# Two graph networks on one core: the order of every engine's work is written out by hand

## The chip, the cores and the metric

The kernel runs on one core of a Trainium2 chip. The metric is the device time of one execution in microseconds (us). A core has five engines with a queue each: PE (matmul), DVE (vector), ACT (scalar), POOL (gathers and scatters by index) and SP (plain DMA issues; ACT issues some too). Each works through its own queue; semaphores tie them together.

## The reference, cut to what matters

There are 6250 nodes with 64 features and 200000 edges sorted by target. First a one-layer graph network updates the nodes, then an edge MLP and three attention layers follow.

```python
# first network, per target node over its edges
e      = leaky_relu(cat([pre_w * z[src], z[dst]]) @ att_w)       # z = x @ Wa
alpha  = softmax of e over the edges of a node
h      = sum(alpha * z[src]);  max_feat = max(pre_w * x[src] @ Wg);  mean_feat = mean(pre_w * x[src])
x      = layernorm(x + sigmoid(cat([x, max_feat, mean_feat]) @ gate_w) * h)
# second network
edge_attr = relu(ln(edge_embed) @ eW1 + eb1) @ eW2 + eb2          # 64 -> 256 -> 64 for every edge
for l in range(3):
    hh    = ln(x)
    alpha = softmax over the edges of (q(hh[dst]) * (kn(hh[src]) + ke(edge_attr)))    # 8 heads of 8
    agg   = sum(alpha * (vn(hh[src]) + ve(edge_attr)))
    gate  = sigmoid(agg @ Wih + hh @ Whh)
    x     = x + (agg + gate * (hh @ Wself - agg)) @ Wout
    x     = x + relu(ln(x) @ mW1) @ mW2
x = layernorm(x + ln(x_second))
```

## The kernel before

The nodes are sorted by degree and cut into 49 blocks (NB) of 128, one node a partition. Block b has CAPS[b] edge slots a node (50 down to 21). There are two stages.

**Stage 1** does the first network and the edge MLP, block by block. `meet` fetches a block's index data (me), own rows (ow) and edge features (xe) by indirect DMA and builds masks. `fetch` gathers one source row a slot (L662, tile g, four buffers). `absorb` is the first network: the products and reductions of the gathered rows on DVE (a_part, L841 and L856), the exponential on ACT (L850), the node update and layernorm, then `prepare`, which normalizes the new rows for layer 0 and makes the key and value rows (p_kv, L561 to L565). `place_rows` writes those rows to the table `tab` by indirect DMA (L537). `even` layernorms the edge features on DVE (f_sm L672, f_sq L678) and stores them. `select` finds, for each node, one edge in each of 16 "windows" of the source numbers (NW = 16), and lists the other edges (LCAPS[b], 40 down to 14). Window edges are later read by one-hot matmuls. It builds the one-hots in four sets: a matmul broadcasts (L743), ACT copies (s_bc, L746), DVE compares three times (s_oh, L749), and SP stores (oh_d, L750). `order` puts a block's edges into the new order on PE: SP loads the stored features (f_xs, L763), DVE makes a selection matrix (f_mv, L775), PE multiplies (f_tr, L781), ACT copies (f_xt, L784). `features` is the edge MLP: f_ph (L818) on PE, f_hid (L821) on ACT, f_pe (L800) on PE, ea (L804) on ACT, stored to ea_d (L805).

**Stage 2** runs the three layers over the blocks in the order ORDER. A layer first loads the whole table's bf16 parts for the window matmuls (ftb, seven DMAs on ACT's queue, L958). `fetch1` loads a block's one-hots (ohl), edge terms (eal), transposed node rows (hv), and node rows (b_x), and gathers the rows of the non-window edges (L986). `attend` takes the edge terms (L1008), the gathered rows through an identity matmul (L1013), or the window rows through one-hots (L1022), into b_pk in PSUM, eight edges a time. ACT copies them out (b_k L1026, b_v L1029), and DVE makes scores (L1031, L1032), softmax and the weighted sum (L1033 to L1043). Then the chain of the node update follows: flip, gate (L1068 to L1075), output projection, layernorm (b_h), flip (p_pm L523), MLP (L1088 to L1094), the new row b_x (L1095), and `prepare` for the next layer. Layer 2 writes the output instead (L1107). The next layer's gathers read a table whose rows must all be written.

Both stages sit in a context `schedule_with_timeline_sim=True`: a scheduler decides, from modelled times, in which order each engine gets its instructions; the program text fixes only what depends on what. The buffer pools decide what may be in flight. In PSUM of stage 1 there are two banks each for f_tr and p_pm, a two-bank f_ph tile, and one bank for f_pe.

Of the kernel before, what the change touches and what calls it, by code (L numbers as in the profile page):

```python
# [9 lines left out]
F32 = mybir.dt.float32  # L10
# [8 lines left out]
H = 8  # L19
# [402 lines left out]
def passes(ctx, tc, ins, out, meta_d, t0_d, own_d, ident, row_f, ones, norm_c, st_i, id_i, off, end, has, hash_, rdeg,  # L422
# [118 lines left out]
    def prepare(wk, mps, w, b, xb, i):  # L541
# [3 lines left out]
        norm(wk, hn, xb)  # L545
        pt = mps.tile([D, P], F32, name="p_pm")
# [7 lines left out]
        if b == 0:  # L554
            nc.sync.dma_start(hd[LB][:, LN:P], ht[:, :SPARE])
        pm = mps.tile([P, W1], F32, name="p_pm")
        nc.tensor.matmul(pm, ht, w["wc"][:, D : 3 * D], start=True, stop=True)
        kv = wk.tile([P, WT], F32, name="p_kv", bufs=3)
        part = kv[:, W1:].bitcast(BF).rearrange("p (k d) -> p k d", k=3)
        rest = wk.tile([P, W1], F32, name="p_rest")  # L560
        nc.scalar.copy(kv[:, :W1], pm)  # L561
        nc.scalar.copy(part[:, 0], pm)
        nc.vector.tensor_tensor(rest, pm, part[:, 0], ALU.subtract)
        nc.scalar.copy(part[:, 1], rest)
        nc.vector.tensor_tensor(part[:, 2], rest, part[:, 1], ALU.subtract)  # L565
# [4 lines left out]
    with tc.tile_pool(name="e1", bufs=1) as wp, tc.tile_pool(name="e_g", bufs=4) as gp, \  # L570
# [3 lines left out]
            tc.tile_pool(name="e_tr", bufs=2, space=PSUM) as tps, \  # L574
            tc.tile_pool(name="e_h", bufs=1, space=PSUM) as hps, tc.tile_pool(name="e_e", bufs=1, space=PSUM) as eps2, \
            tc.tile_pool(name="e_p", bufs=2, space=PSUM) as mps, tc.tile_pool(name="e_f", bufs=1, space=PSUM) as fps:
# [25 lines left out]
        xss = [wp.tile([P, D // 4, D], F32, name=f"f_xs{i}") for i in range(6)]  # L602
# [18 lines left out]
        def meet(b):  # L621

            c, ce = CAPS[b], CAPE[b]
# [6 lines left out]
            xe = xp.tile([P, c, D], F32, name="xe")  # L630
            nc.gpsimd.indirect_dma_start(out=xe.rearrange("p c d -> p (c d)"), out_offset=None, in_=ins["edge_attr_64"][:],
                                         in_offset=bass.IndirectOffsetOnAxis(ap=st_i[:, b : b + 1], axis=0))
            kk, wt = row_f[:, :c], me.bitcast(F32)[:, :, 1]
# [20 lines left out]
            got[b] = dict(me=me, ow=ow, xe=xe, vm=vm, ivm=ivm, am=am1, wg=wg, si=si)  # L654

        def fetch(b):
            m = got[b]
            m["g"] = []
            for k0, k1 in cuts(CAPS[b], b == ORDER[-1]):
                g = gp.tile([P, CH, F0], F32, name="g0")  # L660
                for k in range(k0, k1):
                    nc.gpsimd.indirect_dma_start(  # L662
                        out=g[:, k - k0, :], out_offset=None, in_=t0_d[:],
                        in_offset=bass.IndirectOffsetOnAxis(ap=m["si"][:, k : k + 1], axis=0))
                m["g"].append((k0, k1, g))

        def even(b):
# [5 lines left out]
            nc.vector.tensor_scalar(mr, sm[:, 0], 1.0 / D, None, ALU.mult)  # L673
            nc.vector.tensor_tensor(xe, xe, mr.unsqueeze(2).to_broadcast([P, c, D]), ALU.subtract)
            for k0 in range(0, c, 12):
                k1 = min(k0 + 12, c)
                sq = wk.tile([P, 12, D], F32, name="f_sq")
                nc.scalar.activation(sq[:, : k1 - k0], xe[:, k0:k1], AF.Square)  # L678
                nc.vector.tensor_reduce(sm[:, 1, k0:k1], sq[:, : k1 - k0], AX.X, ALU.add)
# [4 lines left out]
            nc.sync.dma_start(xd_d[b][:], xe)  # L684

        def select(b):
# [12 lines left out]
            nc.vector.tensor_tensor(v, t[:, 0], vm, ALU.mult)  # L699
            me = w1p.tile([P, NW, c], F32, name="s_m")  # L700
# [4 lines left out]
            nc.vector.tensor_reduce(sel, me, AX.X, ALU.max)  # L705
            nc.vector.tensor_scalar(f_sm, sel, 1.0, None, ALU.max)
            nc.vector.tensor_tensor(me, me, f_sm.unsqueeze(2).to_broadcast([P, NW, c]), ALU.is_equal)
            ch, lv, pos = t[:, 1], t[:, 2], t[:, 3]
            nc.vector.tensor_reduce(ch, me.rearrange("p w k -> p k w"), AX.X, ALU.max)
            nc.vector.tensor_sub(lv, vm, ch)  # L710
# [9 lines left out]
            m["tg"] = tg  # L720

            lf = wk.tile([P, lc], F32, name="s_lf")
            for l0 in range(0, lc, 12):
# [5 lines left out]
                nc.vector.tensor_reduce(lf[:, l0 : l0 + n], li, AX.X, ALU.add)  # L729
# [166 lines left out]
        for i in range(NB + 3):  # L896
            if i < NB:
                meet(ORDER[i])
# [911 lines left out]
```

## Time and profile before

| | |
|---|---|
| time, median of 3 runs | 8684.05 us (8675.6 to 8702.06) |
| time of the profiled execution | 8682.54 us |
| its span | 8680.7 us, so 1.84 us lie around it |
| granted PE clock, mean | 0.798 |
| PE busy | 6156.6 us (71%) |
| DVE busy | 5618.3 us (65%) |
| POOL busy | 5163.6 us (59%) |
| ACT busy | 2467.9 us (28%) |
| first gather of layer 0, 1, 2 | 3660, 5410, 7111 us |

The shares are averages over stages that work differently. A table by stage and the waits of that stage say more than the totals. In a line of waits, the engine and line that stood still come first, then what ended the wait, its total in us, the number of times, and the longest. A wait of an engine that isn't the bottleneck costs nothing by itself.

### The profile page before, as it was taken

The page shows a single profiled execution, that of the slowest core. Times are in us where ns is not written, and L with a number is a line of the kernel's source. Part 1 is how long each engine was busy: PE and PEld are TensorE (multiplying, and loading weights), DVE is VectorE, ACT ScalarE, POOL GpSimd, SP SyncE. Part 2 cuts the span into 40 slices and gives each one's busy share as a digit, 9 for nine tenths or more (in the row PEclk, how much of TensorE's full clock was granted, in tenths as well). Part 3 has the DMA queues.
Part 4 walks back from the last instruction along what each step waited for, and adds up shares of the span by engine and source line. Part 5 has one row for each costly group of instructions (what it writes and reads, how often), then busy time and mean ns, then how long its engine had stood idle before and what let it go on. Part 6 is the DMA issues. An engine that isn't in the chain of part 4 may idle for free.

```text
span 8680.7 us, 151284 instructions
## 1 busy us (share of the span) xinstructions
PE 6156.6 (71%) x58020; PEld 4136.1 (48%) x58020; DVE 5618.3 (65%) x13393; ACT 2467.9 (28%) x5210; POOL 5163.6 (59%) x5441
## 2 busy tenths in 40 slices
PE   2455556566565566678778886889888868888897
PEld 1222223233232233355656664566666646666676
DVE  6677667777566576555655665566656646677777
ACT  1233334334333343422222221222222212222222
POOL 4555445555444444377776671777777627777775
PEclk6677777777676677788888887888888868888998
DMA  5444344454343344365555663556666635556664
GB/s 120 121 113 132 109 121 134 124 141 123 110 116 109 108 123 120 105 182 142 146 139 137 150 146 89 142 146 149 152 147 154 143 96 140 139 146 149 152 163 107
DMA packets 965727, 1146.71 MB, mean 132 GB/s; under 512 B 665160, under 2 KB 713109, under 8 KB 957961
## 3 DMA queue, kind: packets, MB, share of 16 engines
q1 hardware_dynamic: 504569, 642.88, 23.9%
q0 software_dynamic: 180144, 412.30, 23.6%
q10 hardware_dynamic: 280288, 81.76, 3.9%
q8 instruction: 466, 7.63, 0.4%
q14 instruction: 260, 2.13, 0.1%
HBM read 899.50 MB, written 236.89 MB: 131 GB/s over the span
## 4 chain that ended last, share of the span: by engine, by line
PE 22%; POOL 14%; DVE 9%; issue 7%; DMA 5%; ACT 1%; ACTq 0%; SPq 0%; POOLq 0%; DVEq 0%
POOL g L986 13%; PE b_pk L1022 7%; PE b_pk L1013 5%; PE b_pk L1008 5%; DMA g<-tab,fidx 3%; DVE b_ag L1043 2%; DVE b_k L1031 2%; DVE b_al L1032 1%; DMA hv<-ht_d 1%; DVE b_v L1042 1%; PE p_pm L1088 1%; PE p_pm L1094 1%; PE p_pm L1092 0%; PE b_qe L997 0%; DVE n_t L501 0%
## 5 line engine op out<-in xcount | busy, mean ns | idle before, releaser
L986 POOL DMA_INDIRECT g<-tab,fidx x3426 | 3273.1, 955 | 1154.5 <-issue 991.7
L662 POOL DMA_INDIRECT g<-ft_d,si x1596 | 1530.0, 959 | 1652.6 <-DVE a_part L856 1152.7
L1022 PE MATMUL b_pk<-ftb,ohl 128*128 128x128 bf16 x21609 | 1409.5, 225 | 63.1 <-DMA ftb<-tab 49.8
L1022 PEld LDWEIGHTS <-ohl 128*128 128x128 bf16 x21609 | 1299.4, 101 | 142.4 <-issue 81.3
L1013 PE MATMUL b_pk<-g,fident 128*128 128x512 f32 (+3 forms) x2148 | 1091.8, 629 | 253.1 <-DMA g<-tab,fidx 227.2
L1008 PE MATMUL b_pk<-fwkv,eal 64*128 64x128 f32 x11556 | 1047.2, 313 | 224.8 <-ACT b_v L1026 223.4
L781 PE MATMUL f_tr<-f_mv,f_xs 128*64 128x40 f32 (+11 forms) x12544 | 576.3, 261 | 817.2 <-DVE f_mv L775 575.8
L1008 PEld LDWEIGHTS b_pk<-fwkv,eal 64*128 64x128 f32 x11556 | 856.6, 210 | 531.8 <-ACT b_v L1026 262.2
L818 PE MATMUL f_ph<-f_xt,fw 64*128 64x448 f32 (+3 forms) x2320 | 736.6, 718 | 471.5 <-ACT f_hid L821 467.5
L781 PEld LDWEIGHTS f_tr<-f_mv,f_xs 128*64 128x64 f32 x12544 | 564.5, 177 | 1024.1 <-DVE f_mv L775 583.0
L1026 ACT COPY b_k<-b_pk 128x512 f32<-128x512 f32 (+3 forms) x753 | 412.1, 547 | 1994.5 <-PE b_pk L1013 1067.5
L1043 DVE TENSOR_REDUCE b_ag<-b_v 128x64 f32<-128x2624 f32 (+18 forms) x147 | 654.6, 4453 | 265.4 <-PE p_pm L523 262.6
L1031 DVE TENSOR_TENSOR b_k<-b_k,b_qe 128x1024 f32<-128x1024 f32 (+11 forms) x402 | 436.4, 1105 | 528.8 <-ACT b_k L1029 233.7
L800 PE MATMUL f_pe<-f_hid,fw 128*64 128x448 f32 (+3 forms) x2320 | 677.7, 666 | 49.6 <-ACT ea L804 25.8
L821 ACT ACTIVATE f_hid<-f_ph,fb 128x896 f32<-128x896 f32 (+3 forms) x580 | 566.6, 977 | 467.6 <-PE f_ph L818 416.0
L1013 PEld LDWEIGHTS b_pk<-g,fident 128*128 128x128 f32 x2148 | 412.3, 221 | 545.2 <-issue 376.8
L818 PEld LDWEIGHTS f_ph<-f_xt,fw 64*128 64x128 f32 x2320 | 217.6, 229 | 702.1 <-ACT f_hid L821 632.6
L749 DVE TENSOR_SCALAR s_oh<-s_bc,f_parts 128x512 bf16<-128x512 f16 x588 | 185.0, 367 | 508.0 <-DMA oh_d<-s_oh 484.2
L784 ACT ACTIVATE f_xt<-f_tr,feg 128x304 f32<-128x304 f32 (+11 forms) x392 | 240.6, 615 | 936.4 <-PE f_tr L781 916.5
L775 DVE TENSOR_TENSOR f_mv<-s_tt,e_fac 128x608 f32<-128x608 f32 (+11 forms) x392 | 311.5, 810 | 217.3 <-PE f_tr L781 202.0
L1032 DVE TENSOR_REDUCE b_al<-b_k 128x128 f32<-128x1024 f32 (+11 forms) x402 | 435.0, 1102 | 3.4
L537 POOL DMA_INDIRECT tab<-p_kv,id_i x147 | 147.4, 1002 | 482.8 <-DVE p_kv L565 356.6
(359 smaller groups left out, 7947.0 us busy)
## 6 DMA issues: line engine op xcount, KB each, us to landing
ohl<-oh_d SPq DMA_DIRECT2D x588, 384.0 KB
eal<-ea_d SPq DMA_DIRECT2D x174, 512.0 KB
oh_d<-s_oh SPq DMA_DIRECT2D x196, 384.0 KB
g<-tab,fidx POOLq DMA_INDIRECT x3426
eal<-ea_d SPq DMA_DIRECT2D x93, 384.0 KB
eal<-ea_d SPq DMA_DIRECT2D x66, 448.0 KB
ea_d<-ea ACTq DMA_DIRECT2D x130, 224.0 KB
g<-ft_d,si POOLq DMA_INDIRECT x1596
```

The costliest lines, as they stand in the source:

```text
L662: nc.gpsimd.indirect_dma_start(out=g[:, k - k0, :], out_offset=None, in_=t0_d[:], in_offset=bass.IndirectOffsetOnAxis(ap=m["si"][:, k : k ...
L781: nc.tensor.matmul(pv[r * D : (r + 1) * D, j], xs[4 * j0 // D][:, (j0 + j) % (D // 4), :], mv[:, j, :, r::2], start=True, stop=True)
L800: nc.tensor.matmul(pe[h * D : (h + 1) * D, :w], w2[:, s, :], hid[s][:, h, :w], start=(s == 0), stop=(s == 1))
L818: nc.tensor.matmul(ph[:, h, :w], w1[r, s * P : (s + 1) * P], xf[r, e0 * D : e1 * D], start=True, stop=True)
L821: nc.scalar.activation(hid[s][:, :, :w], ph[:, :, :w], AF.Relu, bias=b1[:, s : s + 1])
L986: nc.gpsimd.indirect_dma_start(out=g[:, k - k0, :], out_offset=None, in_=tab.rearrange("n (k d) -> (n k) d", d=D), in_offset=bass.Indirect ...
L1008: nc.tensor.matmul(pk[:, j % 2, j // 2, :], ea[r, e, :], w["wkv"][r], start=(j < 2), stop=False)
L1013: nc.tensor.matmul(pk[:, h, :m, :], ident, g[:, u0 - k0 + h : u0 - k0 + n : 2, :], start=False, stop=True)
L1022: nc.tensor.matmul(pk[:, h, j, :], o, tbh[:, cl + NW * u, i, :], start=False, stop=(j == m - 1 and u == us[-1] and i == 2))
L1031: nc.vector.tensor_tensor(k, k, q.unsqueeze(1).to_broadcast([P, k1 - k0, D]), ALU.mult)
L1032: nc.vector.tensor_reduce(al[:, k0:k1], k.rearrange("p k (h d) -> p k h d", h=H), AX.X, ALU.add)
L1043: nc.vector.tensor_reduce(a, vv.rearrange("p k d -> p d k"), AX.X, ALU.add)
```

## The change

Both stages are now inside `tc.manual_schedule()`: every engine gets its instructions in the order of the program text. The text is rewritten so that this order is meant. In stage 1, `absorb`, `even`, `masks` (split off from `meet`) and `select` become generators that yield after a piece, with a weight in us. An iteration has eight steps (STEPS), and each lays down an eighth of the weight, drawn from two jobs (the absorb of block i-2; the even, masks and select of blocks i-1 and i), one `order` step, and two steps of the edge MLP.

```diff
-            tc.tile_pool(name="e_tr", bufs=2, space=PSUM) as tps, \
-            tc.tile_pool(name="e_h", bufs=1, space=PSUM) as hps, tc.tile_pool(name="e_e", bufs=1, space=PSUM) as eps2, \
-            tc.tile_pool(name="e_p", bufs=2, space=PSUM) as mps, tc.tile_pool(name="e_f", bufs=1, space=PSUM) as fps:
+            tc.tile_pool(name="e_tr", bufs=1, space=PSUM) as tps, \
+            tc.tile_pool(name="e_h", bufs=2, space=PSUM) as hps, tc.tile_pool(name="e_e", bufs=1, space=PSUM) as eps2, \
+            tc.tile_pool(name="e_p", bufs=1, space=PSUM) as mps, tc.tile_pool(name="e_f", bufs=1, space=PSUM) as fps, \
+            tc.manual_schedule():
...
-        xss = [wp.tile([P, D // 4, D], F32, name=f"f_xs{i}") for i in range(6)]
+        xss = [wp.tile([P, D // 4, D], F32, name=f"f_xs{i}") for i in range(4)]
...
+        STEPS = D // JB
+        meet(ORDER[0])
+        for i in range(NB + 3):
+            bs = [ORDER[i - k] if 0 <= i - k < NB else None for k in range(4)]
+            if i < NB:
+                meet_features(bs[0])
+            if i + 1 < NB:
+                meet(ORDER[i + 1])
+            jobs = []
+            if bs[2] is not None:
+                jobs.append([absorb(bs[2]), 0.0, 25.0])
+            second = ([even(bs[1])] if bs[1] is not None else []) + ([masks(bs[0])] if bs[0] is not None else []) \
+                + ([select(bs[1])] if bs[1] is not None else [])
+            if second:
+                jobs.append([chain(*second), 0.0, 26.0])
+            total, done = sum(j[2] for j in jobs), 0.0
+            mlp = [features(bs[3], 1) if bs[3] is not None else iter(()), features(bs[2], 0) if bs[2] is not None else iter(())]
+            for s in range(STEPS):
+                b = bs[2]
+                if b is not None:
+                    mv = got[b]["mv"]
+                    if s < STEPS - 1:
+                        aim(b, (s + 1) * JB)
+                half = s * 2 // STEPS
...
+                next(mlp[half], None)
+                while jobs and (done < total * (s + 1) / STEPS or s == STEPS - 1):
...
+                if b is not None:
+                    order(b, s * JB, mv)
+                next(mlp[half], None)
...
+                if s % 2:
+                    n = 4 * (i - 2) + s // 2 + 2
+                    if 0 <= n < 4 * NB:
+                        bring(n)
+            fetch()
+            if bs[1] is not None:
+                aim(bs[1], 0)
+            place_rows(1)
+        place_rows()
```

`bring` holds the f_xs loads, `aim` the f_mv, `order` the f_tr matmuls and the f_xt copy. `fetch` lists the gathers of a block's parts in order and issues as many as tiles are free: a tile counts as free behind the second reduction in `absorb` that reads it, and `fetch` is called there and at the end of an iteration. `place_rows(1)` keeps the last block's rows for the next iteration. The end of `select` reads:

```diff
+                bc = wk.tile([P, 4, P], F16, name="s_bc")
+                nc.scalar.copy(bc, pb)
+                yield 0.2
+                oh = wk.tile([P, 4, 3, P], BF, name="s_oh")
+                for u in range(3):
+                    nc.vector.tensor_scalar(oh[:, :, u, :], bc, parts[:, u : u + 1], None, ALU.is_equal)
+                nc.sync.dma_start(oh_d[b][:, w0 * 3 * P : (w0 + 4) * 3 * P], oh.rearrange("p w u n -> p (w u n)"))
```

In stage 2, `attend` is cut into functions: `sums` (b_pk and its copies, one group), `scores`, `soft`, `values`, `turned`, `gate`, `update`, `updated`, `turned2`, `hidden`, `close`, `more` (the pieces of `prepare`). An iteration takes the sums of block b, the softmax and gate of the block before (b1), the update of b2 and the rest of `prepare` of b3.

```diff
+            for _ in range(3):
+                load()
+            for _ in range(4):
+                load_oh(), gather()
+            for b in ORDER[:2]:
+                ms[b] = begin(b)
+            for i in range(NB + 4):
+                b, b1, b2, b3 = [ORDER[i - k] if 0 <= i - k < NB else None for k in range(4)]
...
+                do(b1, soft)
+                do(b2, updated)
+                if i + 2 < NB:
+                    ms[ORDER[i + 2]] = begin(ORDER[i + 2])
...
+                steps = [lambda: (do(b3, more), do(b1, values)), lambda: (do(b3, more), do(b2, turned2)),
+                         lambda: (do(b3, more), do(b2, hidden)), lambda: (do(b3, more), do(b2, close), do(b1, turned)),
+                         lambda: do(b1, gate), lambda: (do(b2, more), do(b1, update))]
+                done = 0
+                for j, (k0, k1, u0, u1) in enumerate(groups):
+                    if u0 == k0:
+                        m["k"] = wk.tile([P, CL, D], F32, name="b_k", bufs=3)
+                    sums(b, m, k0, k1, u0, u1)
+                    if u1 == k1:
+                        scores(m, k0, k1)
+                        load()
+                        if k0:
+                            gather()
...
+                    while done < len(steps) * (j + 1) // len(groups):
+                        steps[done]()
+                        done += 1
+                for f in steps[done:]:
+                    f()
+                place_rows()
+                put()
```

Smaller edits: the two small copies of p_kv read the SBUF tile instead of PSUM; the MLP's two p_pm tiles become one; groups of sums are balanced in size (a part of 10 edges is two groups of 6 and 4, not 8 and 2); hv has four buffers instead of three, b_x and xv five instead of three; the transposes of `order`'s target list move into `select`.

## The prediction, made before the change was run

> **What bounds the kernel now.** I first read the top of the page: no engine is busy throughout, so the bound differs by stage.
>
> ```profile
> span 8680.7 us, 151284 instructions
> ## 1 busy us (share of the span) xinstructions
> PE 6156.6 (71%) x58020; PEld 4136.1 (48%) x58020; DVE 5618.3 (65%) x13393; ACT 2467.9 (28%) x5210; POOL 5163.6 (59%) x5441
> ...
> PEclk6677777777676677788888887888888868888998
> ```
>
> The timeline of gathers gives the borders. The first network (stage 1) runs from about 240 to 3660 us, where the first row gather of layer 0 starts; the layers follow to 5407, 7108 and 8668. The table by stage, with two stretches of stage 1 and then the three layers, reads (window, then length, PE, PEld, DVE, ACT, POOL busy, granted clock, DMA share, GB/s):
>
> ```profile
> 1736.00:2170.00 434.00, 274.35 (x2582) 140.71 (x2582) 327.31 (x849) 174.18 (x280) 225.27 (x237) 0.76 0.48 132
> 2604.00:3038.00 434.00, 231.07 (x2184) 119.89 (x2180) 260.31 (x752) 140.99 (x241) 185.90 (x194) 0.69 0.39 108
> 3660.00:5407.00 1747.00, 1392.98 (x13464) 1044.75 (x13461) 1002.30 (x2077) 429.24 (x1117) 1137.98 (x1190) 0.85 0.56 139
> 5410.00:7108.00 1698.00, 1400.65 (x13192) 1057.28 (x13192) 1013.20 (x2041) 415.38 (x1097) 1140.83 (x1191) 0.84 0.58 141
> 7111.00:8668.00 1557.00, 1331.65 (x13009) 1010.55 (x13008) 1097.20 (x2580) 363.09 (x901) 1140.84 (x1191) 0.88 0.60 145
> ```
>
> In stage 1 DVE is busiest, at 75% in a good stretch and 60% in a bad one. What it and POOL wait for there (total, times, longest, 220 to 3600 us):
>
> ```profile
> POOL g L662 <- DVE a_part L856: 1152.7, 43, 47.1
> PE f_tr L781 <- DVE f_mv L775: 566.5, 64, 41.7
> DVE s_oh L749 <- DMA oh_d<-s_oh: 473.0, 51, 43.4
> DVE f_sm L672 <- DMA xe<-in_edge_attr_dram,st_i: 292.1, 31, 12.9
> ```
>
> A ring shows: gathers wait for DVE to free a gather tile, DVE stands up to 43 us at a one-hot build for a store queued on SP behind others, and SP's next f_xs load waits its turn. The start of each block's gathers gives the period: 356.46 to 3523.21 us over 44 blocks, 72.0 each, in good stretches 65.1 (1773.5 to 1968.7 is three blocks), in bad ones up to 108.
>
> In the layers POOL issues 1142 row gathers, 0.955 us each and 0.3 behind it, so 1.257 x 1142 = 1435 us, and 49 table writes at about 1.3 (64): a floor of 1500. It stands still beyond that for some 250, 200 and 60 us in layers 0, 1, 2, most at the end of a layer (6860 to 7120 us):
>
> ```profile
> POOL tab L537 <- DVE p_kv L565: 126.5, 8, 27.7
> POOL tab L537 <- DVE b_gt L1075: 44.1, 2, 23.2
> ```
>
> The last sums of layer 1 end at 7023.6, its last table row is written at 7107.8: 84 us of update chains, one after another, about 15.6 us apart, before the next layer's gathers may read.
>
> [...] the 43 us stall at L749 held all later DVE work. So a hand order is a real change, and an instruction that waits blocks those below it. [...]
>
> **Stage 1, part by part.** Removed nothing large: the same 588 one-hot builds, 12544 f_tr and 2320 f_ph matmuls, 1596 gathers. Moved:
>
> (a) Gathers go behind masks and each second a_part reduction, a full iteration ahead. POOL's work is 33.6 x 1.257 + about 4 = 46 us of a block, beside DVE. The 1152.7 us wait mostly had cover on DVE, so I give it no price of its own.
>
> (b) f_xs loads, two issues of about 3.4 us a quarter-block on SP, are brought two steps ahead, past the one-hot stores; two tiles fewer (six to four) are the price. SP's sum is some 38 us a block (eight such issues, four stores of 2.1, small ones), hidden behind DVE if no store waits at its head.
>
> (c) xe is asked for an iteration earlier: 292.1 us of DVE wait, 6 a block, go; POOL's gathers stand ahead of it by 41 us at most, less than an iteration.
>
> (d) DVE in program order. Its busy time in a block is 327.31 / 434 x 65.1 = 49. There were 849 / 434 x 65.1 = 127 operations; in the trace an independent follower starts 82 ns before its predecessor ends, a dependent one 34 ns after it (medians), a difference of 0.116. A hand order puts dependent ones together: at most 127 x 0.116 = 15, at least 0. I take 6: 55.
>
> (e) New stall: the last step of a block holds all four one-hot sets, 12 builds at 0.367. s_oh has two buffers and is freed by its oh_d store, 2.1 us of issue and about 3 of landing on SP, and each set waits for a PE broadcast and ACT copy on the single p_pm bank. Queued behind it: the next f_mv on DVE, so f_tr on PE. Two of four sets wait about 3.3 each: 6.5 (0 to 15).
>
> (f) Other in-order waits (softmax's exp between two DVE operations, f_mv for f_tr): 4 (0 to 12).
>
> So 55 + 6.5 + 4 = 65 us a block, DVE-bound and regular. Beside it, from the same stretch scaled to a block: PE 274.35 / 434 x 65.1 = 41, ACT 26, POOL 46 from (a). 49 x 65 = 3185, with about 90 for the three thinner iterations of start and drain 3275, against 3420: **145 gained** (-150 to +490).
>
> **The layers, part by part.** The update of a block (norm, flips, gate, MLP, close, table row) is cut into six pieces laid between the next blocks' groups of 8 sums; loads and gathers run four tiles ahead. PE per block: 147 window matmuls at 58 ns are 8.5, L1008 1.16 per eight edges, L1013 1.98, updates 6.7: 24 to 27. POOL: 52 us for a block of 40 edges, 29 for 22, 19 for 14. So POOL sets the pace for the first 29 blocks (764 gathers and 29 writes: 999 us); the middle dozen take 324 at about 27, the last eight 25.5 each by PE: 204. Sum 1527; start and drain I put at 80: the first gather-to-sum latency and a drain of three chained update stages, about 45 instead of 84. So **1610 a layer**. Layer 0: 1747 to 1610, +137; layer 1: 1698 to 1610, +88; layer 2: 1557 to about 1587, -30, since it has neither tail and already runs within 4% of POOL's floor. **195 gained** (0 to 330). The low end is a PE-paced 29 us in the small blocks, which adds 45 a layer, and a tail as long as now. p_kv's copies from SBUF, the merged p_pm tile and the balanced groups are single instructions beside POOL: zero, and if PE is the pace less than 0.5 us a block (25 a layer).
>
> **Sum.** 8682.54 (profiled run: span 8680.7 and 1.84 around it; 1.5 under the median 8684.05) - 145 - 195 = 8342, so **8340**. A measurement of this kernel can tell 0.3%, 26 us, from no change.
>
> **The rivals.**
> 1. *Stage 1 reaches DVE's floor.* No set stalls, more overlap: 58 a block, so 49 x 58 + 90 = 2932, 488 gained, beside the same 195. For it: the good stretch above runs at 65 with waits in it. Against: single banks, and four sets in a row. 8682 - 683 = 8000.
> 2. *Slower: the one-hot step blocks DVE.* In a strict order a store landing late on SP, behind f_xs loads of 3.4 us each, holds s_oh, then f_mv, then f_tr, then the single f_tr bank. The break-even is 340 / 49 = 7 us a block above mine, 72. With 75 a block stage 1 takes 3675 + 90, 345 more than now; less 195 it ends at 8830. For it: 43 us stalls of just this wait now. Against: f_xs is asked for earlier and in an order that never waits on a later store.
> 3. *The layers gain nothing:* PE in order waits on ACT's b_k and b_v copies (254 and 223 us in total now), what the tails give is spent there, and stage 1 comes out at 71. About 8680.
>
> **How the numbers follow.** My forecast 0.55 (8340, its own range 8150 to 8560), rival 1 0.29, rival 2 0.12, rival 3 0.04. Faster 0.84, same 0.04, slower 0.12. The range 7930 to 8670 takes in rival 1 and leaves out rival 2.
>
> **What would show it.** Right: the wait of L662's gathers for a_part falls from 1152.7 to under 300 in total, xe's to near nothing; block starts come every 63 to 67 us, evenly; s_oh still waits on its store, 200 to 400 in total, in runs of less than 10; the first layer's gather starts near 3515; from the last sums to the last table row takes about 45. Wrong: a period over 72 with s_oh or f_mv ahead of the idle; layers longer than 1650 with PE's waits on ACT ahead of POOL.

## The result, and the profile after

The changed kernel takes 8546.1 us (median of 4 runs, 8539.47 to 8553.86) where the kernel before took 8683.98 in the same runs: a ratio of 0.9839, with a 95% interval of 0.9821 to 0.9857. It is 138 us faster; 340 were forecast. The profiled execution took 8539.47 us around a span of 8537.4.

The top of the page after:

```profile
span 8537.4 us, 150270 instructions
## 1 busy us (share of the span) xinstructions
PE 6224.1 (73%) x58044; PEld 4258.2 (50%) x58044; DVE 6013.9 (70%) x13393; ACT 2476.6 (29%) x5234; POOL 5161.1 (60%) x5439
```

PE, ACT and POOL are busy about as long as before. DVE's busy time rose by 396 us (5618.3 before), though it has as many instructions. In stage 1 the order does this, not the new text: a later run (e6) gives that text back to the scheduler, and DVE is busy 2297 us in the stage, where the same text by hand (e1) has 2563. In program order dependent operations stand next to each other and overlap less. From 240 us to the first gather of layer 0 the durations of DVE's operations add up to 2749 us before and 2781 after, and overlap took 412 us off that before, 222 after. Of the neighbours on DVE that are under 0.3 us apart (220 to 3600 us), 3247 now read the tile that the one ahead has just written, where it was 910; these start 35 ns after its end (34 before), and those that read and write other tiles 82 ns before it (medians, 82 before).

The table by stage of the changed kernel (window, length, busy time of PE, PEld, DVE, ACT, POOL, granted clock, DMA share, GB/s). The windows run from one first gather to the next, so they are stage 1 and the three layers:

```profile
240.00:3626.00 3386.00, 2073.09 (x17987) 1031.63 (x17987) 2558.97 (x6279) 1246.06 (x2018) 1634.07 (x1705) 0.71 0.46 120
3626.00:5260.00 1634.00, 1354.24 (x13222) 1052.40 (x13218) 1061.44 (x2073) 415.90 (x1109) 1140.45 (x1191) 0.86 0.58 147
5260.00:6899.00 1639.00, 1362.17 (x13200) 1061.67 (x13200) 1060.10 (x2045) 412.15 (x1105) 1140.96 (x1191) 0.85 0.59 148
6899.00:8537.00 1638.00, 1349.34 (x13053) 1060.62 (x13053) 1171.34 (x2580) 359.16 (x909) 1140.73 (x1191) 0.83 0.57 139
```

| gained, us | forecast | measured |
|---|---|---|
| stage 1 (first gather of layer 0 at 3660.2, now 3625.6) | 145 | 34.6 |
| layer 0 (1750.2, now 1635.1) | 137 | 115.1 |
| layer 1 (1700.6, now 1638.8) | 88 | 61.9 |
| layer 2 to the end of the span (1569.6, now 1637.9) | -30 | -68.3 |

So 110 us are missing in stage 1, and 86 in the layers. The waits of stage 1 after (engine and line, releaser, total, times, longest; 220 to 3600 us):

```profile
POOL g L679 <- DVE wx L663: 1026.5, 41, 42.8
...
DVE p_kv L569 <- ACT p_kv L567: 190.3, 42, 8.2
...
DVE s_oh L791 <- DMA oh_d<-s_oh: 167.1, 79, 13.4
...
PE f_tr L825 <- DMA f_xs<-xd_d: 123.2, 17, 15.1
...
DVE p_rest L566 <- ACT p_kv L563: 107.8, 40, 3.5
```

DVE's wait for xe is gone (292.1 before), and that for the one-hot stores fell from 473.0 to 167.1. In their place two other waits have grown: DVE now stands 298 us for ACT's copies p_kv, in the making of the table rows. Of these the kernel before has only one worth a line, and a small one (220 to 3600 us):

```profile
DVE p_rest L563 <- ACT p_kv L562: 7.3, 4, 4.1
```

What the totals hide shows in the start of each block's node update, a_gm, once a block. Over the whole stage the blocks come every 71.6 us before and every 70.1 after. By the block's width (CAPS, slots a node) the mean distance to the block before is:

| width | 43 | 41 | 38 | 37 | 35 | 34 | 33 | 32 | 31 | 30 | 29 | 28 |
|---|---|---|---|---|---|---|---|---|---|---|---|---|
| before, us | 105 | 110 | 79 | 94 | 67 | 72 | 65 | 63 | 86 | 62 | 80 | 63 |
| after, us | 89 | 109 | 75 | 87 | 70 | 69 | 68 | 67 | 75 | 65 | 72 | 63 |

The blocks with a prime width (43, 41, 37, 31, 29) are slow in both kernels. At most other widths from 35 down the changed kernel is the slower one. SP's timeline of the changed kernel, first in blocks of width 31, then of width 33 (start, duration, line, what is issued, how many in a row):

```profile
2332.77 0.34 SPq L792 DMA_DIRECT2D oh_d<-s_oh  x1
2333.21 1.91 SPq L796 DMA_DIRECT2D oh_d<-s_o  x1
2335.21 5.04 SPq L792 DMA_DIRECT2D oh_d<-s_oh  x3
2340.35 22.57 SPq L805 DMA_DIRECT2D f_xs<-xd_d  x4
2363.03 8.13 SPq L712 DMA_DIRECT2D xd_d<-xe  x1
2371.25 11.18 SPq L805 DMA_DIRECT2D f_xs<-xd_d  x2
2382.95 7.59 SPq L944 DMA_DIRECT2D x_d<-a_x  x1
```

```profile
1918.13 4.36 SPq L792 DMA_DIRECT2D oh_d<-s_oh  x3
1922.58 3.65 SPq L805 DMA_DIRECT2D f_xs<-xd_d  x4
1943.56 0.34 SPq L712 DMA_DIRECT2D xd_d<-xe  x1
1943.99 1.21 SPq L805 DMA_DIRECT2D f_xs<-xd_d  x2
```

Four f_xs loads keep SP for 22.57 us at width 31 and for 3.65 at width 33. In the first the queue is busy without a break, and even the store of one small tile (x_d, 0.3 us elsewhere) is held for 7.6. The mean of one f_xs issue by width, over the whole stage: 43: 8.2, 41: 9.1, 37: 6.5, 31: 5.4, 29: 5.0, 23: 4.4; 38: 3.8, 34: 3.6; all others 0.5 to 1.7. The slow ones are the prime widths, and 34 and 38 somewhat. A load of width 31 has 31 x 16 rows of 256 bytes, 127 KB, and where four loads come in a row the later issues stand 6.9 to 7.8 us each, which is 16 to 18 GB/s; at 34 slots the mean is 3.6. The single packets of SP's queue in the trace agree. During four loads in a row at widths 29, 31, 37 and 43, at most 71 packets of 256 bytes pass in a us (18 GB/s) and never more than two are under way at once; at 34 and 38 it is 142 in a us and four at once; at 33 it is 392 to 540 in the densest us, with 12 to 16 under way. Why the width does this the trace does not show.

### The profile page after: what moved, and what is told of

The parts are those of the page before. It is cut to its first block, busy times and chain, and to the rows that moved or that the text cites. A ratio compares the mean times of both kernels' runs of the same rounds, so it can differ in the third digit from the quotient of the medians.

```text
span 8537.4 us, 150270 instructions
## 1 busy us (share of the span) xinstructions
PE 6224.1 (73%) x58044; PEld 4258.2 (50%) x58044; DVE 6013.9 (70%) x13393; ACT 2476.6 (29%) x5234; POOL 5161.1 (60%) x5439
## 5 line engine op out<-in xcount | busy, mean ns | idle before, releaser
L679 POOL DMA_INDIRECT g<-ft_d,si x1596 | 1527.7, 957 | 1625.1 <-DVE wx L663 1026.5
L1101 PE MATMUL b_pk<-ftb,ohl 128*128 128x128 bf16 x21609 | 1375.8, 229 | 19.4 <-DMA ftb<-tab 19.4
L1101 PEld LDWEIGHTS <-ohl 128*128 128x128 bf16 x21609 | 1325.0, 104 | 65.5 <-issue 41.4
L1093 PE MATMUL b_pk<-g,fident 128*128 128x384 f32 (+3 forms) x2172 | 1028.8, 601 | 219.9 <-DMA g<-tab,fidx 180.5
L844 PE MATMUL f_pe<-f_hid,fw 128*64 128x448 f32 (+3 forms) x2320 | 710.7, 700 | 595.1 <-ACT ea L848 594.9
L1105 ACT COPY b_k<-b_pk 128x512 f32<-128x512 f32 (+2 forms) x753 | 404.7, 537 | 2257.9 <-PE b_pk L1101 1252.3
L825 PE MATMUL f_tr<-f_mv,f_xs 128*64 128x40 f32 (+11 forms) x12544 | 603.0, 269 | 510.5 <-ACT f_xt L829 291.9
L844 PEld LDWEIGHTS f_pe<-f_hid,fw 128*64 128x64 f32 x2320 | 143.2, 168 | 1013.3 <-ACT ea L848 760.5
L1105 ACT COPY b_v<-b_pk 128x512 f32<-128x512 f32 (+2 forms) x753 | 410.4, 545 | 0.0
L1130 DVE TENSOR_TENSOR b_v<-b_v,b_qe 128x2624 f32<-128x2624 f32 (+18 forms) x147 | 406.0, 2762 | 0.0
L862 PEld LDWEIGHTS f_ph<-f_xt,fw 64*128 64x128 f32 x2320 | 235.1, 238 | 292.9 <-ACT f_xt L829 147.5
```

The lines of the kernel that those rows point to most:

```text
L679: nc.gpsimd.indirect_dma_start(out=g[:, k - k0, :], out_offset=None, in_=t0_d[:], in_offset=bass.IndirectOffsetOnAxis(ap=got[b]["si"][:, k ...
L825: nc.tensor.matmul(pv[r * D : (r + 1) * D, j], xss[(4 * ORDER.index(b) + 4 * j0 // D) % 4][:, (j0 + j) % (D // 4), :], mv[:, j, :, r::2], ...
L844: nc.tensor.matmul(pe[h * D : (h + 1) * D, :w], w2[:, s, :], hid[s][:, h, :w], start=(s == 0), stop=(s == 1))
L862: nc.tensor.matmul(ph[:, h, :w], w1[r, s * P : (s + 1) * P], xf[r, e0 * D : e1 * D], start=True, stop=True)
L1093: nc.tensor.matmul(pk[:, h, :c, :], ident, g[:, u0 - k0 + h : u0 - k0 + n : 2, :], start=False, stop=True)
L1101: nc.tensor.matmul(pk[:, h, j, :], o, tbh[:, cl + NW * u, i, :], start=False, stop=(j == c - 1 and u == us[-1] and i == 2))
```

## Experiments

Each run stood beside the kernel before on the same chip, and its ratio is to that kernel. The runs were made on several chips, on which the kernel before took between 8671 and 8698 us, so a difference of some 25 us between two rows can be the chip; the ratios take that out. "By hand" means under the hand order, "planned" under the scheduler, "split" with the loads of e1. A stage or layer ends with the first gather of the next one, or with the span.

| run | stage 1 | layer 0 | layer 1 | layer 2 | median, us | ratio (95%) |
|---|---|---|---|---|---|---|
| before | 3660 | 1750 | 1701 | 1570 | 8684 | 1 |
| after | 3626 | 1635 | 1639 | 1638 | 8546 | 0.9839 (0.9821 to 0.9857) |
| e1 after, split loads | 3462 | 1636 | 1642 | 1642 | 8388 | 0.9644 (0.9628 to 0.9661) |
| e2 after, b_h2t first | 3632 | 1610 | 1615 | 1641 | 8499 | 0.9767 (0.9751 to 0.9783) |
| e3 before, split loads | 3382 | 1753 | 1711 | 1571 | 8421 | 0.9680 (0.9664 to 0.9696) |
| e4 after, late norms | 3623 | 1638 | 1649 | 1629 | 8542 | 0.9819 (0.9803 to 0.9836) |
| e5 split, mixed blocks | 3454 | 1593 | 1567 | 1553 | 8169 | 0.9421 (0.9405 to 0.9437) |
| e6 split, stage 1 planned | 3271 | 1634 | 1643 | 1638 | 8190 | 0.9447 (0.9431 to 0.9463) |
| e7 split, late rows | 3121 | 1637 | 1646 | 1639 | 8044 | 0.9274 (0.9256 to 0.9292) |
| e8 old stage 1, split, new stage 2 | 3359 | 1654 | 1646 | 1639 | 8300 | 0.9572 (0.9555 to 0.9589) |
| e13 all together | 3125 | 1540 | 1544 | 1556 | 7766 | 0.8935 (0.8920 to 0.8950) |
| e14 late rows, not split | 3358 | 1634 | 1639 | 1638 | 8276 | 0.9522 (0.9506 to 0.9537) |
| e15 split, stage 2 planned | 3465 | 1573 | 1572 | 1566 | 8173 | 0.9397 (0.9382 to 0.9413) |
| e16 split, width 32 as 31 and 1 | 3512 | 1643 | 1639 | 1638 | 8434 | one run |
| e17 after, both planned | 3560 | 1571 | 1576 | 1558 | 8267 | 0.9508 (0.9492 to 0.9524) |
| e18 as e13, stage 2 planned | 3133 | 1555 | 1556 | 1556 | 7791 | 0.8959 (0.8944 to 0.8974) |

My theory after the result was: stage 1 lost its gain to the loads of prime width, and the layers lost some of theirs to PE's waits in program order. The rival for stage 1: DVE with its own waits is the bound everywhere, and the loads are hidden.

### The loads

e1 splits the load of the poor widths; e3 does it in the kernel before (L763).

```diff
-                nc.sync.dma_start(xss[n % 4][h * D : h * D + c], xd_d[b][...][h::2].rearrange("j k d -> k j d"))
+                r = 32 if c >= 32 else 16
+                for k0, k1 in ((0, r), (r, c)) if c in (23, 29, 31, 34, 37, 38, 41, 43) else ((0, c),):
+                    nc.sync.dma_start(xss[n % 4][h * D + k0 : h * D + k1], xd_d[b][...][h::2, k0:k1].rearrange("j k d -> k j d"))
```

> The changed kernel with each f_xs load of a block whose width is 23, 29, 31, 34, 37, 38, 41 or 43 slots issued as two (32 or 16 slots, and the rest). In the trace these widths take 3.6 to 9.1 us of SP for one issue, all others 0.5 to 1.7. Theory A (the expected gain of stage 1 was lost in these blocks, where SP's loads set the period, 70 to 108 us): issues fall to about 1 us, these 17 blocks run at the pace of their neighbours, stage 1 ends 110 us earlier (60 to 150), and the whole takes about 8435 us. Theory B (stage 1 is bound by DVE with its waits for ACT and the one-hot stores in every block): the issues get shorter, but the blocks do not, stage 1 within 25 us of now, 8520 to 8550.

Measured: all f_xs issues together fall from 939 to 357 us, and stage 1 ends 164 us earlier. The issues of the changed kernel and of e1 (number, then shortest, median and longest in ns):

```profile
L805 SPq DMA_DIRECT2D f_xs<-xd_d x392: 218/708/16539, 154.1 to 3601.4; - x196
L807 SPq DMA_DIRECT2D f_xs<-xd_d x528: 230/450/4882, 157.0 to 3430.3; - x176
```

Width 41 goes from 109 to 71 us a block, 37 from 87 to 74, 31 from 75 to 65, 29 from 72 to 64. Widths 34 and 38 don't move (69 and 75): so their issues of 3.6 to 3.8 us were hidden already. Theory A holds, with a gain a little over its range; B falls as a statement about these blocks.

> The kernel before with the same split of the f_xs loads. Theory A (in both kernels SP's loads hold the blocks of these widths): stage 1 gets at least 100 us shorter here too, more than in the changed kernel, since the one-hot stores that DVE waited for (473 us in all) stand behind these loads: 8684 to about 8540. Theory B (the hand order's stage 1 wins just because it hides these loads better): 8684 to 8650 or more.

Measured: 277 us faster, stage 1 from 3660 to 3382, and the wait for the one-hot stores goes from 481.5 to 48.5 us. So the loads held both kernels, the old one more. With short loads the changed stage 1 (3462) is 80 us slower than the old one (3382). So the 35 us that the change gains in stage 1 come from standing the slow loads better, and with these mended it is a loss.

> The changed kernel with split f_xs loads, and the loads of the four blocks of width 32 issued as 31 slots and 1 instead of 32. The bytes are the same. Theory A [...]: the 31-slot issues take 4 to 6 us instead of 0.6, these four blocks take 72 to 77 us instead of 67. Theory B (it is the size of the block or the place in time): issues under 1.5 us, 67 us.

```diff
-... if c in (23, 29, 31, 34, 37, 38, 41, 43) else ((0, c),):
+... if c in (23, 29, 31, 34, 37, 38, 41, 43) else ((0, 31), (31, 32)) if c == 32 else ((0, c),):
```

Measured: the four blocks of width 32 take 78.0 us instead of 67.2. The 31-slot issue itself is short (0.35 us); the 1-slot issue behind it stands 8.33. So A is right that the width does it, with the bytes the same, and a detail of it was wrong: the long record in SP's row is not that of the slow load but of the issue after it. The changed kernel's timeline above has the same: the four loads of width 31 at 2340 us stand 0.27, 7.84, 6.90 and 7.37 us, and the store of xe behind them 8.13; behind the next two loads the store of x_d stands 7.59. The trace shows the time, not the reason.

### The table rows

e7 takes the making of a block's rows (prepare) out of the end of absorb and gives it to the next iteration as a job of its own, spread over eight steps; e14 is the same without the split loads.

```diff
-            for _ in prepare(wk, mps, nxt, b, xb, 0):
-                yield 1.5
+            preps[b] = prepared(b, xb)        # the same loop as a generator
...
-                jobs.append([absorb(bs[2]), 0.0, 25.0])
+                jobs.append([absorb(bs[2]), 0.0, 19.0])
+            if bs[3] is not None:
+                jobs.append([preps.pop(bs[3]), 0.0, 6.0])
```

The reason is in DVE's timeline of the changed kernel (start, duration, line, operation, the idle time before it and what ended it):

```profile
1773.47 0.29 DVE L566 TENSOR_TENSOR p_rest<-p_kv 128x128 f32<-128x128 f32 x1 [2.67 <-ACT p_kv L563]
...
1778.97 0.29 DVE L569 TENSOR_TENSOR p_kv<-p_rest,p_kv 128x128 bf16<-128x128 f32 x1 [4.41 <-DMA g<-ft_d,si]
1780.11 0.88 DVE L791 TENSOR_SCALAR s_oh<-s_bc,f_parts 128x512 bf16<-128x512 f16 x3 [0.84 <-ACT s_bc L787]
...
1783.90 0.88 DVE L791 TENSOR_SCALAR s_oh<-s_bc,f_parts 128x512 bf16<-128x512 f16 x3 [1.86 <-DMA oh_d<-s_oh]
1785.46 1.04 DVE L791 TENSOR_SCALAR s_oh<-s_bc,f_parts 128x512 bf16<-128x512 f16 x3 [0.68 <-DMA oh_d<-s_oh]
```

p_rest and p_kv are two operations of 0.29 us, and DVE stands 7.1 us for them: each needs a copy of ACT just made, and these copies come late from ACT, which has other work in its queue. (At the second the profile names a gather here; in 42 of the blocks it is ACT's copy L567.) The one-hots, which I had feared more, cost 3.4 here.

> The changed kernel with split f_xs loads, and in stage 1 the making of a block's table rows (prepare) laid out over the next block's eight steps instead of at the end of its own. Theory A (DVE is the bound, and 300 us of its idle time are the waits for ACT's p_kv copies in these rows, 6.3 us a block): these waits fall under 60, stage 1 from 3462 to about 3230, total about 8160. Theory B (the waits move elsewhere: DVE then meets the one-hot stores or f_tr sooner): half of that or less, 8280 to 8370.

Measured: stage 1 falls by 341 us, to 3121. The waits of DVE in it (220 to 3100 us):

```profile
DVE s_oh L791 <- DMA oh_d<-s_oh: 107.8, 86, 3.2
DVE f_sm L702 <- ACT f_sq L697: 42.7, 47, 0.9
DVE s_oh L791 <- ACT s_bc L787: 29.1, 34, 3.7
```

The p_kv waits no longer show, and little took their place: DVE is busy 2542 of 2880 us, 88%. Theory A, and more than it said. The gain exceeds the 303 us of these waits in e1, because the wait for ACT's s_bc fell too, from 87.7 to 29.1; the wait for f_sq is new, and that for the stores stays (96.7 in e1).

> The changed kernel with late table rows in stage 1, but with the f_xs loads as they were. Theory A (two separate bounds: the blocks of prime width are held by SP's loads whatever the order, the others by DVE with its waits for p_kv): the other blocks gain the 7 to 10 us that they gain with split loads, the prime ones (43, 41, 37, 31, 29) little, together 230 of the 340 us: 8546 to about 8310. Theory B (the late rows free SP, DVE and ACT alike): 8250 or less.

Measured: 267 us less in stage 1, 8276 in all. Width 33 goes from 67.5 to 59.3 us, but 37 only from 87 to 85, 31 from 75 to 72, 29 from 72 to 70. The total lies between the two forecasts, but the widths speak for A: two separate bounds. The split is worth 164 us with early rows and 237 with late ones, as if a block is held by the longer of the two.

### The layers

The gathers of a layer run at POOL's floor (956 ns for one and 0.3 us behind it, 1142 times, and 49 table writes of 1.0 and 0.3 us: about 1500 us): they take 1510, 1513 and 1508 us of the three layers (1581, 1531 and 1495 before). The rest is what follows the last gather, the drain: 125, 125 and 130 us (169, 170 and 75 before). POOL's timeline at the end of layer 0:

```profile
5137.07 0.98 POOL L537 DMA_INDIRECT tab<-p_kv,id_i  x1 [0.30 <-issue]
5150.98 0.98 POOL L537 DMA_INDIRECT tab<-p_kv,id_i  x1 [12.93 <-DVE p_kv L569]
5182.33 0.97 POOL L537 DMA_INDIRECT tab<-p_kv,id_i  x1 [30.37 <-DVE p_kv L569]
5212.81 0.97 POOL L537 DMA_INDIRECT tab<-p_kv,id_i  x1 [29.51 <-DVE p_kv L569]
5236.75 0.97 POOL L537 DMA_INDIRECT tab<-p_kv,id_i  x1 [22.98 <-DVE p_kv L569]
```

A small block is gathered in 19 to 27 us and summed in 30, so sums lag until the gathers are four tiles ahead. In the 30 us PE waits 5.7, 4.0 of it at one place: PE's timeline, then ACT's:

```profile
5177.90 0.27 PE L523 MATMUL p_pm<-fident,b_h 128*64 128x128 f32 x1
5182.14 0.60 PE L1188 MATMUL p_pm<-b_h2t,fm 64*128 64x128 f32 x3 [3.96 <-ACT b_h2t L528]
```

```profile
5178.59 0.59 ACT L1105 COPY b_v<-b_pk 128x512 f32<-128x512 f32 x1
5181.43 0.30 ACT L567 CAST p_kv<-p_rest 128x128 bf16<-128x128 f32 x1 [2.25 <-DVE p_rest L566]
5181.63 0.45 ACT L528 ACTIVATE b_h2t<-p_pm,fnrm 64x128 f32<-64x128 f32 x1
```

b_h2t was ready to be copied at 5178.2. Its copy stands on ACT behind the p_kv copy of another block, that one waits for DVE's p_rest, and p_rest stands on DVE behind scores that wait for ACT. PE, at the end of this, stands still. e2 exchanges the two calls:

```diff
-lambda: (do(b3, more), do(b2, turned2)),
+lambda: (do(b2, turned2), do(b3, more)),
```

> The changed kernel with the two calls of the second of the six update steps exchanged, so that on ACT the copy b_h2t of the block before last stands ahead of the p_kv copy of the block before that one, which waits for DVE. Theory A (PE in order stands 4.0 us a block at the MLP matmul L1188 for b_h2t, and this sets the 30.4 us period of the last twenty blocks of layers 0 and 1): the wait goes, these blocks take 26 to 27 us, layers 0 and 1 each 40 to 80 us shorter, layer 2 as before; total about 8430. Theory B (another wait of PE takes its place, b_gt or the copies of b_k, or DVE's 22 us plus its own waits are the pace): layers within 15 us of 1634 each, total 8520 to 8550.

Measured: layers 0 and 1 are 26 and 24 us shorter, between the two theories. In the last blocks of layer 0 PE's longest wait at L1188 falls from 4.0 to 1.4, and the last twenty blocks of both layers come every 29.2 us instead of 30.1. About half of the gain is in the drain (14 and 11 us), half in the gathers, which now take 1499 and 1500. So this wait is a part of the slow pace and not most of it.

In layer 2 there are no rows to make, and PE stands 4.2 us at another place (PE's timeline):

```profile
8458.82 0.43 PE L1172 MATMUL p_pm<-fbr,fones 1*128 1x64 f32 x2
8463.43 0.49 PE L1173 MATMUL p_pm<-fwout,b_gt 64*128 64x64 f32 x2 [4.18 <-DVE b_gt L1166]
```

DVE does the two last layernorms of another block ahead of b_gt. e4 turns them into two late pieces (the norm with its scale and bias, then the last norm), as prepare's are.

```diff
-                y = wk.tile([P, 2, D], F32, name="b_y", bufs=3)
-                norm(wk, y[:, 0], xb)
-                ...
-                last.append((b, n, y))
+                m["next"] = finish(b, m)      # the same operations as a generator with one yield
```

> The changed kernel with layer 2's two last layernorms (b_y, some 22 DVE operations, 5.7 us) taken out of the step that closes a block and laid in two pieces behind the later steps. Theory A (in layer 2 PE stands 4.2 us a block at L1173 for b_gt, which stands on DVE behind these norms, so the last blocks take 29.5 us): the wait falls to about 1 us, the last twenty blocks take 26 to 27 us, layer 2 goes from 1642 to about 1580, layers 0 and 1 as before; total about 8485. Theory B (DVE's sum of work is the pace of layer 2): no more than 15 us gained.

Measured: PE's wait for b_gt halves (42.9 to 19.6 us in 8200 to 8440), yet layer 2 gains 9 us, in all 8542: no difference that a run can tell. The gain is within B's 15 us, but B's reason, DVE's sum of work, isn't shown: from 8000 to 8400 us DVE is busy 73% of the time before the edit and 74% after it, and under the scheduler (e15) the same blocks take 26.1 us. The edit brought a wait of its own. It keeps the tile b_y longer, and DVE then stands for the output store that frees it, 46.4 us in e4 where it was 9.4 (8000 to 8440 us):

```profile
DVE b_y L518 <- DMA out_dram<-b_y,id_i: 46.4, 4, 27.2
```

So this run settles neither theory; b_y with more buffers was not tried.

e5 leaves all this and changes which blocks meet: large and small in turn.

```diff
+ORDER2 = tuple(b for k in range(NB // 2) for b in (k, LB - k)) + (NB // 2,)    # used in stage 2 for ORDER
```

> The changed kernel with split f_xs loads (8388 us, layers 1636, 1642, 1642), and in the three layers the blocks taken large and small in turn (0, 48, 1, 47, ...) instead of large to small. Theory A (large blocks are bound by POOL's gathers, small ones by PE with its waits at 30 us, so the gathers run at POOL's floor of 1510 us and then four blocks of 30 us are still to be summed): mixed, the four tiles of lead even it out, the gathers still take about 1510, and the drain falls from 125 to 60 to 80: 45 to 65 us a layer, total 8200 to 8250. Theory B (the drain is the depth of the update pipeline, three blocks whatever their size, or PE's sum is the bound): layers within 15 us of now, total 8350 to 8400.

Measured: 43, 75 and 90 us less; drains of 70, 69 and 57, with the gathers at 1524, 1498 and 1496. Theory A, and somewhat more than it said. Blocks paced by POOL's gathers and blocks paced by the sums on PE are interleaved here, and it is worth 208 us over the three layers.

### The order itself

Four runs (e6, e15, e17 and e18) take the hand order off and leave the new text, its buffers and leads.

```diff
-            tc.manual_schedule():       # stage 1 (e6), stage 2 (e15), both (e17)
```

> The changed kernel with split f_xs loads, and stage 1's hand order taken off: same text, pools and buffers, but the scheduler lays out stage 1 again (stage 2 stays by hand). Stage 1 takes 3462 us by hand with split loads; the kernel before with split loads takes 3382. Theory A (the order itself costs it: dependent DVE work side by side, DVE standing 300 us for ACT's p_kv copies and 180 for one-hots): about 3390. Theory B (the new text does: one bank each for f_tr and p_pm, gathers and loads asked for elsewhere): 3440 or more.

Measured: stage 1 takes 3271 us, 191 less than by hand and some 90 to 110 less than the old text planned (3359 in e8 on the same chip, 3382 in e3). Neither theory: here the order costs 191, and the new text, with its single banks, is better for the scheduler than the old. DVE is busy 266 us less than in e1, and its waits for the p_kv copies are 30.3 us together:

```profile
240.00:3271.00 3031.00, 1891.97 (x17889) 970.61 (x17891) 2297.42 (x6214) 1215.91 (x2012) 1626.84 (x1698) 0.75 0.49 134
```

It isn't that any hand order loses: with late rows (e7) stage 1 by hand takes 3121. The text of e7 was not given to the scheduler.

> The kernel before in stage 1 (scheduler's order, with split f_xs loads, 3382 us), with the changed kernel's stage 2 by hand. If the two stages' times are independent, 3382 + 4915 = 8297, 90 below the changed kernel with split loads; theory A says so: stage 1's hand order loses 80 us against the scheduler once the loads are short, stage 2's wins 110. Theory B (the stages share something: the clock that PE is granted, or SP's queue at the border) puts it over 8350.

Measured: 8300, stage 1 at 3359, and stage 2 18 us longer than in e1, all of it in layer 0. The stages are independent to within that.

> The changed kernel with split f_xs loads (8388 us; layers 1636, 1642, 1642), stage 2's hand order taken off: same text, pools and pieces, but the scheduler lays out stage 2 again, stage 1 stays by hand. Theory A (the hand order is what shortened layers 0 and 1 by 115 and 62 us, through drains of 125 instead of 170, and lengthened layer 2 by 68): layers near the old 1750, 1700, 1570; total about 8490. Theory B (the text did it: more buffers for hv, b_x and xv, loads and gathers four tiles ahead, balanced groups): layers within 20 us of 1640 each or shorter, and total 8390 or less.

Measured: layers of 1573, 1572 and 1566 us, some 70 shorter than by hand. Theory B: the new text made the gain, the order lost part of it. Which part of the text (buffers, leads, balanced groups) no run tells. The last twenty blocks come every 26.7, 26.7 and 26.1 us, where by hand it is 30.1, 30.1 and 29.9. POOL's waits in its layer 0 (3500 to 5038 us):

```profile
POOL g L1069 <- issue: 325.7, 1065, 1.4
POOL tab L537 <- DVE p_kv L569: 28.5, 4, 17.9
POOL tab L537 <- DVE n_y L505: 27.4, 3, 15.0
```

The drain is 76 us, and little but the issue gap is left.

> The changed kernel as it stands (f_xs loads not split) with the hand order taken off in both stages: the scheduler lays out the new text with its new buffers. Theory A (the whole gain of 138 us comes from the text: more lead of loads and gathers, more buffers, pieces; the hand order costs time in both stages): layers 1573, 1572, 1566 as in the run with stage 2 planned, stage 1 between 3400 and 3560 (3271 with split loads, and 165 to 280 more as both kernels showed); total 8110 to 8270. Theory B (the hand order is what hides the slow loads, so without it the old stalls return in full): stage 1 over 3600, total over 8310.

Measured: 8267 us. The change without its hand order is 423 us faster than the kernel before, with it 138. The layers are those of e15. Theory A, though stage 1, 3560, is at the upper end of its forecast, and a part of what B named is there: without the order the one-hot stores are a wait of 232.0 us with stalls of up to 34.9, and xe returns with 326.2.

> The changed kernel with split f_xs loads, late table rows in stage 1, blocks mixed in stage 2, b_h2t ahead of p_kv, and layer 2's norms laid out later. Theory A (the gains have separate places: stage 1 at 3120, layers 1593, 1567, 1553 from the mixed order, and some 10 to 20 a layer more from the two reorderings): 7780 to 7830. Theory B (mixed, the layers are at POOL's floor of 1500 plus a drain, and the two reorderings find nothing left): 7830 to 7860.

e13 joins e7, e5, e2 and e4. Measured: 7766 us, 0.8935 of the kernel before, a little better than A. Drains are 46, 50 and 61 us: with the gathers at 1494 a layer, that is nearly all there is.

> The kernel of all gains together (7766 us: stage 1 3124, layers 1540, 1545, 1556) with stage 2's hand order taken off, blocks still mixed. Theory A (mixed blocks and the scheduler heal the same thing, the run of small blocks that lags behind the gathers): layers within 15 us of these, total 7740 to 7800. Theory B (they add up): layers about 1510, near POOL's floor, total 7650 to 7700.

Measured: 7791 us, layers of 1555, 1556, 1556: planned and by hand are now within 15 us. Theory A: the mixed blocks and the scheduler mend the same lag.

The kernels of e13 to e16 had first been run on another chip. There the kernel before took 12692 us, and those of e15, e13 and e14 took 0.9915, 0.9909 and 1.0063 of it (e16, one run: 12865 us). What made that chip slow covers what the edits do, so these four runs are not used for the questions above; but the gains did not show there.

## Why the prediction was right or wrong

**Stage 1, (b), the f_xs loads: wrong, and it decided the stage.** I took one price, 3.4 us an issue, put SP's sum at 38 us a block, and called it hidden behind DVE. That price is the mean of the slow stretch from 2604 to 3038 (3.46), where the median is 0.48: it mixes issues of 0.5 us with ones of 5 to 9. In the eleven blocks of width 43, 41, 37, 31 and 29 the loads alone take SP 40 to 73 us a block, stores are held behind them, and SP is the bound; the split showed 164 us. The sign stood in the profile before: the stretches of up to 108 us that I quoted come at these widths, and I put them down to the ring of waits that they start.

**(f), other in-order waits, 4 us a block: mis-sized.** The p_kv waits alone were 6.1 (298 us over 49 blocks). I had named softmax's exp and f_mv; the pair of copies that go from DVE to ACT and back I had costed at nothing. Taking them away gave 341 us with split loads, 267 without.

**(d), DVE in program order: right.** DVE is busy 2559 / 49 = 52 us a block; I took 55. Against the scheduler's order of the same text (e6 beside e1) it is 266 / 49 = 5.4 more; I took 6. **(e), the one-hot step: right in sum**: 167.1 for the store and 84.7 for ACT, 5.1 us a block against 6.5, though the store's issue of 2.1 us was misread (0.32 in the median before). **(c), xe: right**, that wait is gone. **(a)** had the right effect by another way: POOL's wait is still 1026.5 us, now for the masks (wx), and DVE's list of waits in the stage has a single one for a gather, 4.4 us.

**The sum of stage 1: two errors that partly cancel.** The period came out at 70.1 us a block, not 65; with split loads it is 66.9, so the loads are 3.2 of the 5 missing. But 5 us over 49 blocks are 250, and only 110 are missing in the time. The rule "49 blocks and 90 us, in the 3420 us from 240 on" adds up too much: for the kernel before, at 71.6, it gives 3598. The first gathers stand at 137 us, ahead of where I began to count, which explains a part of it. (Rival 3's 71 a block has the same slip: by this rule it is 3569, not the 3420 of now.) So the length of stage 1 was nearer to its forecast than its period, and that was luck.

**The layers: the mechanism right, the pace of the small blocks mis-sized.** Cut at the start of the weighted sum (b_ag) of the 29th and of the last block, the three parts of a layer are:

| us | forecast | layer 0 | layer 1 | layer 2 | before |
|---|---|---|---|---|---|
| start and the first 29 blocks | 35 + 999 = 1034 | 1003 | 1003 | 1002 | 1084, 1038, 1002 |
| the last twenty | 324 + 204 = 528 | 603 | 603 | 599 | 611, 609, 524 |
| the last updates | 45 | 29 | 33 | 38 | 55, 54, 44 |

(The forecast's 80 for start and drain is parted here into 35 and 45.) POOL's pace held. I took PE's 27 and 25.5 us for the small blocks as if PE never waited; by hand they take 30.1, by the scheduler 26.7. I had written that a PE in program order can wait, as a bound of 29 us and 45 us a layer; it was the case, not the bound. The chain of updates was right and better than forecast: from the last sums to the last table row it takes 35.1 us in layers 0 and 1, where I had 45, and 84 before. In these two layers the start and the last updates came out 47 and 43 us cheaper than forecast and hid most of the 75 that the last twenty blocks lost, which is luck again. Layer 2 lost 68, not 30, by the same pace: the scheduler had taken its last twenty at 26.2 us before.

**The rivals.** Rival 2 had the mechanism by name (a store or load late on SP, behind f_xs issues) and a break-even of 72 us a block. It was so in the eleven blocks, not in 49, and did not turn the sign. Rival 1's 58 us a block in stage 1 needed two edits that are not in the change; with them (e7) the mean is 59.5. Rival 3 misread one of its numbers: 223 us is PE's wait for ACT's copy b_v, but 254 is ACT's wait for DVE. That the order itself might be the loss, and the text around it the gain, was none of my cases. e17 shows it was so.

## What to carry to other kernels

Before a queue's price is taken from a mean, split it by shape: one issue's duration by block width would have shown the bound of stage 1 in one view. An order by hand asks that every pair of operations that crosses to another engine and back be laid apart; two copies side by side cost 6 us a block here, and laid into the next block's steps they left no wait. And a hand order comes with new buffers and leads: take the order off again and measure, before it gets the credit.

## What the runs showed of the hardware that I had not expected

A load over 31 partitions, 16 rows of 256 bytes each, moved at 16 to 18 GB/s, and the cost appears on the queue's next issues: in the run that cut 32 into 31 and 1, the one-slot issue took 8.33 us and the 31-slot one 0.35 (means of 32). A store of 32 KB behind such a load was held 7.6 us as well.

On one chip the kernel before took 46% longer, 12692 us against 8690. In one layer there (4866 to 7433 us) the kernel of e13 took 2567 us, where layers 0 and 1 take 1540 and 1544 on the other chip. DMA moved 93 GB/s in it, against 155 and 157, and from 5000 to 8000 us PE stood 1029 us before the one-hot matmuls, 827 times and up to 3.9 us, without a wait that the profile shows. The engines beside PE were busy about as long as on the other chip (DVE 1056 us against 1061 and 1061, ACT 412 against 408 and 406, POOL 1139 against 1140 and 1140), and a gather's issue on POOL took 0.95 us on both. What was wrong with it I can't tell.
